# A two-layer graph kernel: the last feature chain in a fixed order, and ring places by age

## The chip, the cores and the metric

The kernel runs on one NeuronCore of a Trainium2 chip. The metric is the time of one execution on the device in microseconds (us), as the median of several runs. Lower is better. The engines are PE (TensorE: matmuls, with PEld for its weight loads), DVE (VectorE), ACT (ScalarE), POOL (GpSimd) and SP (SyncE, which here issues all the transfers). Each engine works through its own instructions in order; semaphores tie the engines together.

## The reference

There are 4096 nodes with 64 features each, and a dense 4096 x 4096 matrix `adj` in which about one entry in 128 is not zero.

```python
# layer 0: two hops with tanh
h = jnp.maximum(_layernorm(x), 0.0)
for k in range(2):
    agg = adj @ h
    h = jnp.tanh(jnp.concatenate([agg, h], axis=1) @ W[k])
x = x + h
# layer 1: each row weights its last 100 nonzeros by powers of 1/2, by rank
h = jnp.maximum(_layernorm(x), 0.0)
support = h @ weight
mask = (adj != 0)
rank = jnp.cumsum(mask, axis=1); deg = rank[:, -1:]; k = jnp.minimum(deg, 100.)
pos = rank - (deg - k)
w = mask * jnp.where(pos > 0, 0.5 ** (k - pos), 0.0)
x = x + w @ support + bias
```

So `adj` (64 MB in float32) takes part three times: in hop 1, in hop 2, and in layer 1 through the ranks of its nonzeros alone. Hop 2 needs hop 1's result, and layer 1 needs that of hop 2.

## The kernel before, in words

The nodes are cut into four chunks of 1024 (`NCH`), each of eight blocks of 128. All products are computed transposed: one matmul takes a block's features (64 or 128 columns) as its stationary operand and streams 512 columns of the matrix.

**Sweep 1** (up to about 195 us) reads the whole matrix, two blocks of sources at a time. PE makes hop 1 and as much of hop 2 as the order allows. DVE and ACT turn each nonzero into a byte, and a running count along the sources gives each nonzero its rank, kept as a byte "code" in SBUF, so that layer 1 needn't read the matrix again.

**Sweep 2** (`sweep2`) has three kinds of work, which one planner interleaves.

1. *Blocks.* What hop 2 still lacks, 72 blocks of 128 sources x 1024 targets, is read again, 512 KB per block, by SP (line 813), and multiplied (line 256, two matmuls a block, which the profile records as four). The blocks of target chunks 3 and 2 come first (24 blocks), then 24 of chunk 1, then 24 of chunk 0. A block lands in one of the places of a ring. There are six places, `ring_all`; from block 20 on there are four (`slots`), since the other two become buffers for layer-1 weights. Blocks take the places in turn, `slots[seq % len(slots)]`, and a transfer can't be issued before PE has read the block that had the place. SP issues strictly in order.
2. *The feature chain* of a chunk (`finish_x2`, a generator with four stops), once its last block is in: ACT copies the sums (S, line 540); PE multiplies them with the hop's weights (py, 548); DVE adds (554); ACT takes tanh (558); DVE adds the residual, sums and centres (561, 189, 190); ACT squares (191); DVE sums and scales (193, 194); POOL takes the power -1/2 (195); DVE normalises and splits the features into a high and a low part (198, 582, 583: `feat`); POOL adds the bias (587). The work between two stops goes into the engines' queues together, and what the planner puts in between stands between them in the queues.
3. *Layer 1.* There are 128 units of work (target chunk g, source chunk J, block n of eight), in the order J = 3, 2, 1, 0. A unit needs a weight tile (128 x 1024) made from the codes. `convert` makes it, either by one exponential on ACT (line 656) or by two operations on DVE (648 and 651). PE then makes two matmuls (695) of `feat` of source chunk J with it, so a unit must wait for the features of its source chunk. After eight units the sums of a target chunk are added to `parts` in SBUF (`evict`, lines 724 to 731), and for J = 0 they are multiplied by the layer's weights (746), added (751) and stored (753). The last 56 units (`n_late`) are left for the time after the last block, 24 of them with J = 1 and 32 with J = 0, and the 32 need the features of chunk 0.

The planner is Python at build time. It keeps a clock for each engine, adds an assumed duration for every piece (`use`), and from these clocks decides what comes next: `fill` puts pairs of units into gaps in which it expects PE to wait for a block, `decode` makes weights ahead of need as long as ACT's clock is not over PE's by more than `state["lead"]`, or, for DVE, PE's by more than 1.0, and as long as a next step of the chain isn't held up (`end`). What it decides is fixed in the program; at run time every engine just follows its own order. After the last block a loop makes a chain step when it is due, then a unit if its features are ready on the clock, and `decode` after each.

Of the kernel before, what the change touches and what calls it, by code (L numbers as in the profile page):

```python
# [43 lines left out]
def gnn_kernel(  # L44
# [46 lines left out]
    def place(shape, dtype, tag, name):  # L91
        return cpool.tile(shape, dtype, tag=tag, name=name)
# [404 lines left out]
    clock = {"PE": 0.0, "DVE": 0.0, "ACT": 0.0, "POOL": 0.0, "DMA": 0.0}  # L497

    def use(engine, us, after=0.0):
        clock[engine] = max(clock[engine], after) + us  # L500
        return clock[engine]
# [97 lines left out]
    def space(ap, t=0.0, until=None):  # L599
        if until is not None:  # L600
            lent[until] = ap
        if not any(ap is v for v in gone):
            spaces.append((ap, t))
# [5 lines left out]
    def pair_space(tag, *ts):  # L609
        v = place([P, 2, CW], F32R, tag, "weights")  # L610
        for r in range(2):
            space(v[:, r, :], ts[r % len(ts)])
# [13 lines left out]
    ready = {}  # L626
    made = []
    done = {}
    chain = []
    state = {"done": 0, "lead": 5.0, "dve": False}  # L630

    def convert(engine=None):
        i = len(made)
# [26 lines left out]
    def decode():  # L660
        while True:
            ahead = len(made) - state["done"]
            now = clock["PE"] + state["lead"]

            end = max(chain[0][0], clock["PE"]) + 0.4 if chain and ahead > 3 else 1e9
            t = min((v[1] for v in spaces), default=1e9)
            act, dve = (max(clock[e], t) for e in ("ACT", "DVE"))
            if len(made) == len(units):
                act = dve = 1e9
            if state["dve"] and dve + 1.4 < act + 1.05 and dve <= min(clock["PE"] + 1.0, end - 1.4):  # L670
                convert("DVE")
            elif act <= min(now, end - 1.05):
                convert("ACT")
            elif settled and clock["DVE"] <= clock["PE"] + 1.5 and (
                not chain or max(clock["DVE"], clock["PE"]) <= max(chain[0][0], clock["PE"]) + 0.3
            ):
                J, g, s = settled[0]
                settle()
                done[J, g] = use("DVE", 1.25)
            else:  # L680
                return

    def layer1(n):

        for i in range(state["done"], min(state["done"] + n, len(units))):
            state["done"] += 1
            while len(made) <= i:
                convert()
            J, g, k = units[i]
            if k == 0 and g not in sums:  # L690
                sums[g] = pacc.tile([P, NC, C], F32, tag="acc", name="accl")
            first, last = k == 0 and (J + 1, g) not in kept, k == CB - 1 and (J, g) not in kept
            w = made[i][0]
            for c in range(NC):
                nc.tensor.matmul(  # L695
                    sums[g][:, c, :], feats[J][:, k, :], w[:, c * C : (c + 1) * C],
                    start=first, stop=last,
                )
            space(w, use("PE", 0.45, max(made[i][1], ready[J])) + 0.2)
            if k < CB - 1:  # L700
                continue
            t = clock["PE"] + 0.2

            if (J, g) == (NCH - 1, 1):

                give_back("bits")
                state["dve"] = True
            if 0 < J < NCH - 1 or J and g % 2:
                pair_space(f"code{g}{J}", t)
            elif J:  # L710
                parts[g // 2] = place([P, 2, NC, C], F32, f"code{g}{J}", "parts")
            if (J, g) in kept:
                continue
            t = evict(J, g, sums.pop(g))
            if J == 0:
                outs.append((t + 0.1, partial(finish_out, g, part(g))))
# [39 lines left out]
    def sweep2(acc):  # L756
        rings = sorted(range(RING // 2), key=lambda k: places[k][2])
        ring_all = [(k, r) for k in rings for r in range(2)]
        accs = {}
        space(place([P, CW], F32R, "hx0", "weights"), 0.0, "bits")  # L760
        plan = [(2, 16, 20), (3, 24, 32), (2, 20, 32), (1, 16, 32), (1, 8, 16), (0, 8, 32)]
        blocks = [(I, b) for I, b0, b1 in plan for b in range(b0, b1)]
        firsts = dict((v[0], v) for v in reversed(blocks))
        lasts = dict((v[0], v) for v in blocks)
        free = {s: 3.5 * (n // 2 - 2) for n, s in enumerate(ring_all)}
        slots = ring_all
        last = finish_last(acc)
        next(last)
        clock["DMA"] = -7.0
        total = len(blocks)  # L770
        n_late = 7 * CB

        def run_chain(now):
            if chain and chain[0][0] <= now:
                t, gen = chain.pop(0)
                t = next(gen, None)
                if t is not None:
                    chain.insert(0, (t, gen))
                return True
            return False  # L780

        def due(done_blocks):

            return (len(units) - n_late) * (done_blocks - 20) / (total - 20)

        def fill(s):

            while True:
                i = state["done"]
                if (  # L790
                    i + 2 > len(units) - n_late or units[i][0] not in ready or len(made) < i + 2
                    or max(ready[units[i][0]], made[i + 1][1]) > clock["PE"] + 0.3
                    or max(clock["DMA"], free[s]) + 1.33 + 2.2 < clock["PE"] + 0.9
                ):
                    return
                layer1(2)
                run_chain(clock["PE"])
                decode()

        seq = 0  # L800
        for n in range(0, total, 2):
            I, b = blocks[n]
            if n == 20:
                slots = ring_all[:4]
                pair_space(f"ring{rings[2]}", *(free[s] for s in ring_all[4:]))
            if I not in accs:
                accs[I] = two(name="acc1") if I == 1 else plow.tile([P, C], F32, tag="low", name="acc1")
            fill(slots[seq % len(slots)])
            for r in range(2):
                s = slots[seq % len(slots)]  # L810
                seq += 1
                a = ring[s[0]][:, s[1], :]
                nc.sync.dma_start(a, adjA[I, NB - 1 - b - r])
                landed = use("DMA", 1.33, free[s]) + 2.2
                agg_pair(accs[I], at(b + r)[:, D:], a, (I, b + r) == firsts[I], (I, b + r) == lasts[I])
                free[s] = use("PE", 0.9, landed)
            next(last, None)
            if (I, b) == (2, NB - 2):
                give_back(I)
            if (I, b + 1) == lasts[I]:  # L820
                gen = finish_x2(I, accs[I])
                chain.append((next(gen), gen))
            run_chain(clock["PE"])
            if I == 0:
                state["lead"] = 10.0
            decode()
            while state["done"] < min(due(n + 2) + 6, len(units) - n_late):
                i = state["done"]
                J = units[i][0]
                if J not in ready or max(ready[J], made[i][1] if len(made) > i else 1e9) > clock["PE"] + 0.3:  # L830
                    break
                layer1(1)
                run_chain(clock["PE"])
                decode()
        for k in rings[:2]:
            pair_space(f"ring{k}", free[k, 0], free[k, 1])
        while state["done"] < len(units) or chain or outs:
            if run_chain(clock["PE"]):
                decode()
                continue  # L840

            if len(outs) > 1 or outs and state["done"] == len(units):
                t, make = outs.pop(0)
                use("PE", 0.0, t)
                make()
                continue
            i = state["done"]
            if i < len(units) and units[i][0] in ready and ready[units[i][0]] <= clock["PE"] + 1.0:
                layer1(1)
                decode()  # L850
                continue
            decode()
            later = [x[0] for x in chain[:1]] + [t for t in ready.values()]
            clock["PE"] = min(t for t in later if t > clock["PE"])

    sweep2(sweep1())


# [25 lines left out]
```

## Time and profile before

| | us |
|---|---|
| median of 3 runs (374.27 to 376.18) | 374.89 |
| profiled execution | 377.52 |
| its span, first to last instruction | 375.6 |
| PE busy | 342.3 (91%) |
| DVE busy | 294.4 (78%) |
| ACT busy | 199.8 (53%) |
| POOL busy | 24.5 (7%) |
| mean granted PE clock | 0.979 |
| layer-1 matmuls, line 695, x254 recorded | 68.1 |
| weights on ACT, line 656, x92 | 96.8 |
| weights on DVE, lines 648 and 651, x35 each | 24.2 + 25.4 |
| block transfers of 512 KB, issue to landing (median) | 5.0 |

A row of the profile's list of groups is one line, engine and operation: its busy time, the mean of one instruction in ns, and then the idle time of the engine just before, with what ended it. In a line of the timeline, the start comes first, then the time that the merged instructions span, then engine, line, operation, tiles and number. The bracket is the idle time before it and what ended that. A wait for several semaphores is put down to the one that came last, which can be a coincidence. Times in a trace count from the span's start.

### The profile page before, as it was taken

The numbers are of one execution on the slowest core, as the hardware profiler recorded it, in microseconds if no ns is written. First come the engines' busy times: TensorE is split into PE (matmuls) and PEld (weight loads), VectorE is DVE, ScalarE is ACT, GpSimd is POOL, SyncE is SP. The second block draws the span as 40 slices with busy tenths as digits, with TensorE's granted clock in tenths as the row PEclk, the third lists the DMA queues.
The fourth block names the chain that finished last, engine by engine and source line by source line (L and its number), as shares of the span: only waits on it lengthen the run. The fifth ranks groups of instructions, "written<-read, shape, count | busy, mean of one in ns | idle before, by whom it ended". The sixth has DMA issues, their size and how long they took to land.

```text
span 375.6 us, 3973 instructions
## 1 busy us (share of the span) xinstructions
PE 342.3 (91%) x1356; PEld 154.7 (41%) x1356; DVE 294.4 (78%) x524; ACT 199.8 (53%) x226; POOL 24.5 (7%) x21
## 2 busy tenths in 40 slices
PE   3787789999999999999999987988999999995996
PEld 0242224334343443444443421323355544364785
DVE  4999989399989999799989648678167667759863
ACT  2287981674266442530004314085979299928990
POOL 2221100000000000000000004012000030003000
PEclk9999999999999999999999999799999999999798
DMA  8999999999995977849889897978877789800002
GB/s 266 412 410 408 407 411 408 409 410 409 409 367 199 374 305 251 320 171 337 296 335 315 290 366 261 344 240 286 305 257 243 258 301 306 311 38 0 3 28 84
DMA packets 29827, 108.45 MB, mean 289 GB/s; under 512 B 2416, under 2 KB 2800, under 8 KB 29808
## 3 DMA queue, kind: packets, MB, share of 16 engines
q1 hardware_dynamic: 29808, 108.21, 77.5%
q8 instruction: 10, 0.16, 0.2%
q14 instruction: 9, 0.07, 0.1%
HBM read 107.15 MB, written 1.05 MB: 288 GB/s over the span
## 4 chain that ended last, share of the span: by engine, by line
PE 72%; DMA 18%; SPq 4%; ACT 4%; issue 1%; DVE 0%; ACTq 0%
PE acc L468 22%; PE accl L695 16%; PE acc L256 15%; PE acc_low L256 10%; DMA ring<-in_adjA_dram 9%; DMA codes<-in_adjA_dram 8%; SPq L428 3%; PE po L208 3%; PE pto L746 2%; PE pt L324 2%; ACT weights L656 1%; ACT codes L229 1%; PE pt L319 1%; ACT codes L230 1%; PE py L548 1%
## 5 line engine op out<-in xcount | busy, mean ns | idle before, releaser
L656 ACT ACTIVATE weights<-codes,zero 128x1024 fp32r<-128x1024 uint8 x92 | 96.8, 1136 | 6.7 <-PE accl L695 6.2
L256 PE MATMUL acc<-ring,hx 128*64 128x512 f32 x288 | 73.7, 626 | 10.1 <-DMA ring<-in_adjA_dram 10.0
L695 PE MATMUL accl<-weights,feat 128*128 128x512 f32 x254 | 68.1, 414 | 4.2 <-ACT weights L656 4.2
L468 PE MATMUL acc<-ring,hx 128*128 128x512 f32 x152 | 66.1, 593 | 0.0
L695 PEld LDWEIGHTS accl<-weights,feat 128*128 128x128 f32 x254 | 47.2, 195 | 32.2 <-ACT weights L656 12.2
L256 PE MATMUL acc_low<-codes,hx 128*64 128x512 f32 x224 | 53.4, 599 | 7.2 <-DMA codes<-in_adjA_dram 5.5
L468 PEld LDWEIGHTS acc<-ring,hx 128*128 128x128 f32 x152 | 28.6, 190 | 37.1 <-issue 36.5
L250 DVE TENSOR_SCALAR cnt<-codes 128x512 uint16<-128x512 uint16 x128 | 37.6, 294 | 4.4
L249 DVE TENSOR_TENSOR codes<-mbuf,cnt 128x512 uint16<-128x512 uint16 x90 | 38.4, 427 | 3.1
L256 PEld LDWEIGHTS acc<-ring,hx 128*64 128x64 f32 x288 | 17.1, 139 | 53.0 <-DMA ring<-in_adjA_dram 31.7
L195 POOL TENSOR_TENSOR s<-s,half 128x8 f32<-128x8 f32 (+2 forms) x9 | 17.9, 1990 | 313.5 <-DVE s L194 313.5
L396 DVE TENSOR_TENSOR codes<-codes,after 128x2048 uint16<-128x2048 uint16 x32 | 37.7, 1218 | 0.0
L651 DVE TENSOR_SCALAR weights<-bits 128x1024 fp32r<-128x1024 f32 x35 | 25.4, 726 | 15.0 <-PE accl L695 10.8
L230 ACT ACTIVATE codes<-codes 128x1024 uint8<-128x1024 int8 x32 | 33.8, 1057 | 1.0
L256 PE MATMUL acc_low<-ring,hx 128*64 128x512 f32 x96 | 26.8, 679 | 7.9 <-DVE hx L198 6.2
L238 DVE TENSOR_SCALAR mbuf<-ring 128x2048 uint8<-128x2048 f32 x27 | 32.9, 1220 | 0.8 <-DMA ring<-in_adjA_dram 0.6
L229 ACT ACTIVATE codes<-codes 128x1024 int8<-128x1024 f32 x24 | 25.1, 1048 | 14.7 <-DMA codes<-in_adjA_dram 14.7
L256 PEld LDWEIGHTS acc_low<-codes,hx 128*64 128x64 f32 x224 | 15.2, 136 | 38.3 <-issue 25.7
L648 DVE TENSOR_SCALAR bits<-codes 128x1024 uint32<-128x1024 uint8 x35 | 24.2, 691 | 4.8 <-PE accl L695 4.0
L238 DVE TENSOR_SCALAR mbuf<-codes 128x2048 uint8<-128x2048 f32 x21 | 25.6, 1220 | 0.0
L289 ACT CAST mbuf<-mbuf 128x1024 bf16<-128x1024 uint8 x1 | 1.0, 1044 | 37.7 <-DVE mbuf L288 37.7
L724 DVE TENSOR_TENSOR parts<-accl,parts 128x512 f32<-128x512 f32 x16 | 10.3, 684 | 9.7 <-PE accl L695 9.7
(87 smaller groups left out, 244.5 us busy)
## 6 DMA issues: line engine op xcount, KB each, us to landing
ring<-in_adjA_dram SPq DMA_DIRECT2D x74, 512.0 KB, 5.0
codes<-in_adjA_dram SPq DMA_DIRECT2D x33, 1024.0 KB, 14.8
ring<-in_adjA_dram SPq DMA_DIRECT2D x30, 1024.0 KB, 6.2
pre<-in_x_dram SPq DMA_DIRECT2D x4, 256.0 KB, 7.3
xres<-in_x_dram SPq DMA_DIRECT2D x4, 256.0 KB, 5.8
out_dram<-o SPq DMA_DIRECT2D x3, 256.0 KB, 2.5
out_dram<-o SPq DMA_DIRECT2D x2, 128.0 KB, 2.0
wb<-in_weights_dram SPq DMA_DIRECT2D x1, 192.0 KB, 17.2
```

The source lines that it names most:

```text
L229: nc.scalar.activation(sign, a[:, r], AF.Sign)
L230: nc.scalar.activation(m, sign, AF.Square, scale=float((FLAG - 1 + 0.25) ** 0.5))
L238: nc.vector.tensor_scalar(m, a, 0.0, float(FLAG - 1), op0=ALU.not_equal, op1=ALU.mult)
L249: nc.vector.tensor_tensor(q, marks[r].bitcast(U16), cnt, op=ALU.add)
L250: nc.vector.tensor_scalar(cnt, q, 0x7F7F, None, op0=ALU.bitwise_and)
L256: nc.tensor.matmul(acc[c * D : (c + 1) * D, :], src, a[:, c * C : (c + 1) * C], start=first, stop=last,)
L396: nc.vector.tensor_tensor(q, q, a[:, None, :].to_broadcast([P, 4, CW // 2]), op=ALU.subtract)
L468: nc.tensor.matmul(acc[0][:, c, :], at(g), a[:, r, c * C : (c + 1) * C], start=g == CB * I - 1, stop=g == 0,)
L648: nc.vector.tensor_scalar(state["bits"], q, float(ZERO), ONE, op0=ALU.subtract, op1=ALU.mult)
L651: nc.vector.tensor_scalar(w, state["bits"].bitcast(F32), 2.0 ** (127 - LOW), None, op0=ALU.mult)
L656: nc.scalar.activation(w, q, AF.Exp, scale=LN2, bias=zero)
L695: nc.tensor.matmul(sums[g][:, c, :], feats[J][:, k, :], w[:, c * C : (c + 1) * C], start=first, stop=last,)
```

## The change

There are four edits, all in the planner of sweep 2.

1. When the ring shrinks to four places at block 20, the four are put in the order in which they were last used, and the count starts again, so block 20 takes the oldest place.
2. During the last chunk's blocks, the lead that ACT may have in making weights shrinks with the number of blocks left, at most 10 and down to nothing.
3. After the last block, the chain of chunk 0 is written out by hand: two units, one weight conversion on ACT, the chain up to tanh, three units, two conversions on ACT, two parts of the chain (up to the power on POOL), three units, and the rest of the chain.
4. After that the planner goes on with a lead of 3 for ACT and 2 for DVE, and DVE may also convert on its clock up to the moment at which the features of chunk 0 are ready.

```diff
-    state = {"done": 0, "lead": 5.0, "dve": False}
+    state = {"done": 0, "lead": 5.0, "dve": False, "dlead": 1.0, "free": 0.0}
...
-            if state["dve"] and dve + 1.4 < act + 1.05 and dve <= min(clock["PE"] + 1.0, end - 1.4):
+            if state["dve"] and dve + 1.4 < act + 1.05 and dve <= min(max(clock["PE"] + state["dlead"], state["free"]), end - 1.4):
                 convert("DVE")
...
             if n == 20:
-                slots = ring_all[:4]
+                slots = ring_all[2:4] + ring_all[:2]
+                seq = 0
                 pair_space(f"ring{rings[2]}", *(free[s] for s in ring_all[4:]))
...
             if I == 0:
-                state["lead"] = 10.0
+
+                state["lead"] = min(10.0, 1.1 * (total - 3 - n))
...
         for k in rings[:2]:
             pair_space(f"ring{k}", free[k, 0], free[k, 1])
+
+        ((_, gen),) = chain
+        chain.clear()
+        state["lead"] = 10.0
+        layer1(2)
+        convert("ACT")
+        next(gen)
+        layer1(3)
+        for _ in range(2):
+            convert("ACT")
+        next(gen)
+        next(gen)
+        layer1(3)
+        next(gen, None)
+        state.update(lead=3.0, dlead=2.0, free=ready[0])
         while state["done"] < len(units) or chain or outs:
             if run_chain(clock["PE"]):
                 decode()
```

## The prediction

> **What bounds the kernel now.** I read the page first (span 375.6 us, PE 91% busy), then the busy time in stretches of 25 us. From 75 to 200 and from 275 to 300 us PE is busy all of the time, from 300 to 325 for 24.97 of 25 us. It loses time at 200 to 275 (1.86 + 3.58 + 3.35 us) and at 325 to 350 (5.50 us): around the two places that the diff touches. Lines of PE in order of time, first hole:
>
> ```profile
> 230.37 1.08 PE L256 MATMUL acc<-ring,hx 128*64 128x512 f32 x4 [0.15 <-DMA ring<-in_adjA_dram]
> 233.60 1.97 PE L256 MATMUL acc<-ring,hx 128*64 128x512 f32 x4 [2.15 <-DMA ring<-in_adjA_dram]
> 236.48 4.52 PE L256 MATMUL acc<-ring,hx 128*64 128x512 f32 x12 [0.91 <-DMA ring<-in_adjA_dram]
> ```
>
> One block of the second sweep is x4. Counted from 0, the lines are blocks 19, 20, and 21 to 23. Block 20 waits 2.15 us, block 21 waits 0.91, and both lines run slow: 1.97 us where a block takes 1.08, 4.52 where x12 took 2.79 at 224.89. The columns of the stretches are the stretch, its length, busy PE, PEld, DVE, ACT, POOL, then PE's clock, DMA share, GB/s:
>
> ```profile
> 234.00:236.00 2.00, 1.57 (x4) 0.00 (x0) 1.93 (x3) 0.00 (x0) 0.73 (x1) 0.50 0.88 313
> 238.00:240.00 2.00, 2.00 (x8) 0.56 (x8) 1.87 (x2) 0.00 (x0) 0.00 (x0) 0.50 0.93 364
> 348.00:350.00 2.00, 2.00 (x6) 1.52 (x6) 1.75 (x4) 2.00 (x3) 0.00 (x0) 0.50 0.03 8
> ```
>
> After each hole PE runs at half clock. Second hole, in order of time:
>
> ```profile
> 331.45 0.59 ACT L540 COPY S<-acc 128x512 f32<-128x512 f32 x1 [2.13 <-PE acc L256]
> ...
> 335.80 0.69 DVE L554 TENSOR_TENSOR y<-py,pre 128x512 f32<-128x512 f32 x1 [3.65 <-PE py L548]
> 336.40 1.28 DVE L724 TENSOR_TENSOR parts<-accl,parts 128x512 f32<-128x512 f32 x2
> ...
> 340.30 26.10 ACT L656 ACTIVATE weights<-codes,zero 128x1024 fp32r<-128x1024 uint8 x25
> ...
> 343.95 1.79 DVE L651 TENSOR_SCALAR weights<-bits 128x1024 fp32r<-128x1024 f32 x1
> 345.67 0.68 DVE L198 SCALAR_TENSOR_TENSOR xc<-xc,s 128x512 f32<-128x512 f32 x1
> 346.38 0.43 DVE L582 TENSOR_SCALAR feat<-xc 128x512 fp32r<-128x512 f32 x1
> 346.84 0.69 DVE L583 SCALAR_TENSOR_TENSOR feat<-xc,feat 128x512 fp32r<-128x512 f32 x1
> ...
> 347.68 9.83 PE L695 MATMUL accl<-weights,feat 128*128 128x512 f32 x32 [4.18 <-ACT weights L656]
> ```
>
> The chain of chunk 0's features runs from the last block (T = 331.40) to 347.53; PE idles from 343.50 to 347.68. The profile puts that on ACT, but the weights of that unit are the third of the 25 conversions, done about 343.5; the features' end fits. Then x32 takes 9.83 us where the same number at full clock takes 7.44 (x16 in 3.72), so the clock costs 2.4.
>
> **The Trainium skill.** "TensorE: Matmul & The Clock Gate", Part 1, says that PE's clock falls to half after an idle window of about 3.4 us and needs about as long busy to recover. The trace agrees on the half (0.50) and on the hole of 4.18 us, but the first fall came after only 2.15 us of idleness; so I count a gap of 2 us or more as costing clock, about 2.5 us each time as in both holes, and the 1.59 us gap before block 31, at clock 1.00, as not. "SBUF — State Buffer", SBUF: two separate sides, says that VectorE and GpSimd lock a port pair for a whole instruction; here L651 takes 1.79 us in place of 0.69 while POOL's L587 runs (343.94, 1.26 us), and L198 takes 1.74 beside it in an earlier chunk. "DMA: Bandwidth & Descriptors", Anatomy of one DMA, fits 2.0 us plus bytes over 436 GB/s, for another queue than SP: 3.2 us for 512 KB. The shortest landing of L813 is 3.2, the median 5.0.
>
> **Part 1, ring places by age.** Six places shrink to four at block 20. Before, block 20 takes the place that block 18 has just had (read until 230.2), so its transfer is issued at 230.25 and lands at 233.55; 21 waits for 19, and 22 and 23, whose places are long free, queue behind them on SP. After, 20 and 21 take the places of 14 and 15, read by 225.97 and 226.83. Landings of blocks 12 to 19 are 1.27 us apart (221.42 to 230.32 in seven steps), so 20 and 21 land about 231.6 and 232.8, 22 and 23, issued when 18 and 19 end, at 234.1 and 235.4. Block 23 ends about 236.5, not 241.0. No operation is added; the order of units and blocks behind it moves, because the planner's clock does. The gaps stay under 0.3 us, so I take the clock as full.
>
> From there to block 41 (274.70 before) the waits before were 2.15 + 0.91 + 1.27 + 0.17 + 1.59 + 0.14 + 0.17 = 6.4 us and the slow clock 0.89 + 1.73 = 2.6, together 9.0. After, stepping on with 0.93 us a block, 0.465 a unit (x16 in 3.72 is eight units) and 3.3 to 5.7 us from issue to landing, I find: blocks 20 to 23 wait 0.7, 24 and 25 (now ahead of the first units, behind a 256 KB residual load) 1.1, 30 and 31 1.6, 36 to 41 0.2: 3.6. That leaves 5.4. From there to T PE waited only for blocks 57 (0.03), 70 and 71 (0.64 + 0.69), and the last pattern stays. In the new order blocks 52 to 55 stand together with one pair of units behind them, so a place is asked for again after some 3.7 us where landing takes 3.3 to 5.2: waits of about 0.5 before 54 and 55 and 1.0 before 56 and 57. **T comes 5.4 - 1.5 = 3.9 us earlier.** Bounds: 0 if landings of 5 us after issue fill every new gap; 6.5 if hardly a new gap opens; a gap of 2 us would take 2.5 more.
>
> **Part 2, the chain in fixed order.** Before, T to the end of the span is 375.60 - 331.40 = 44.2 us. After, PE has 2 units, py, then 3 + 3. In us after T: S 0.64; py 0.93 to 1.95; y 2.64; tanh 3.30; pre, sum and xc 5.47 (0.72 each with its start; the 1.28 of L724 no longer lies between); ACT puts one conversion between S and tanh and two between tanh and square, ending at 5.45; square 6.13; sum and s 7.05; POOL 1.95 and 0.15 to reach it: 9.15, with L724 x2 in DVE's gap. Then xc: L587 starts with it, so I take 1.74, not 0.68: 10.95; L582 and L583: 12.15. Before, the same point was 16.1. The DVE conversions that stood in the chain (L648 and L651 at 339.65 to 345.7) move behind it. PE's 24 units and py need 24 x 0.465 + 0.93 = 12.1, so the hole closes, worth 4.2 plus 2.4 of clock.
>
> But 41 conversions are then still due (87 of 128 made at T) where 38 were, because the lead shrinks in the last blocks and DVE makes none until 12.15. ACT: 3 in the gaps, then 26 from 6.15 at 1.044 (25 in 26.10): the last ends at 33.4. DVE: one before T, then 11 at 1.53 (L648 at 348.97 to 350.50), with L724 x2 (1.28, two pairs) and one L751 (0.69) among them: the last at 32.2. PE, taking each unit when its weights are there, with the two readings-out of 1.82, stops briefly at the DVE ones (97, 99, 101, 112, 119) and ends its last unit at 35.3, not at 30.5 as bare work gives; before it was 368.59 - 331.40 = 37.2. Then as before 3.77 + 0.45 + 2.79 to the span's end: 42.3. **The tail gains 1.9**, with bounds 0 (another 1.9 us of conversion) and 6.7 (PE never waits: 30.5 + 7.0 = 37.5).
>
> Cost at nothing: fixing the order and naming ACT add no instruction. In T's stretch the conversions hide under PE's blocks; were that cover gone, one is 1.04 on ACT.
>
> Sum: 3.9 + 1.9 = 5.8 us off the profiled span, 375.6 to 369.8. The profiled execution took 377.52 us, 2.6 above the median; the saving taken off the median of 374.89 gives **369.1**.
>
> **Rivals.** (a) The ring gives nothing back: later landings eat it. For it: places are asked for again 3.7 us after their release, and second transfers of a pair took 4.4 to 5.9 us to land (block 29: 5.85). Against it: the 14 pairs of blocks 42 to 69 waited 0.03 us in all. Then only the tail: about 372.8. (b) Conversions don't bind the tail, if ACT and DVE run ahead further than I step: 3.9 + 6.6 = 10.5, so 364.4. Against it: ACT was busy without a break for 26.1 us before. (c) Slower: PE comes to wait on DVE's conversions in the tail. They share an in-order queue with evictions that wait for PE, and the number of units ahead falls from 13 to 17 to 4 to 8, so each wait is passed on. Before, this buffer hid them. My DVE step is (32.2 - 12.15) / 11 = 1.82 us per conversion; at 2.35 it eats the 5.8 us, and at 2.6 the time is 378. For it: DVE's evictions waited for PE for 9.7 us in all before. Against it: ACT makes 21 of the last 32 in its own queue, whatever DVE waits for. (d) Neither hole is worth much, since other waits end at the same moment: 374.
>
> **How the numbers follow.** My case 0.52 (its own range 367.0 to 371.3), (a) 0.18, (b) 0.18, (c) 0.06, (d) 0.06. Within 0.5% (1.9 us, about what this kernel's measurement can tell from no change) lie (d) and a ninth of (a): 0.08; slower 0.06; faster 0.86. The range, 363.9 to 372.9, leaves out (c), (d) and parts of (a) and (b).
>
> **What would show it.** Block 20 starts within 0.3 us of block 19, the clock stays at 1.0 from 232 to 240, block 23 ends near 236.5; short waits before blocks 31 and 54 to 57. L583 of the last chunk ends 12 us after the last block; no hole of 4 us and no half clock behind it; instead PE waits under 1 us each on DVE's L651; ACT's conversions run to 2 us before PE's last unit. I am wrong if block 24 or the pairs behind it wait as long as 20 did, if the clock halves in the tail, or if PE's last unit ends more than 37 us after T.

## The result, and the profile after

The changed kernel took 371.62 us (median; 369.38 to 374.35) against 374.71 us for the kernel before (372.32 to 379.08). The ratio is 0.9917, with a 95% interval from 0.9891 to 0.9943. The change made the kernel faster, by 3.1 us where 5.8 were forecast. The time lies inside the range, 2.5 us above the forecast, 0.3 above the top of the range that I gave for my own case, and 1.2 below rival (a).

| us | before | after |
|---|---|---|
| profiled execution | 377.52 | 370.68 |
| its span | 375.6 | 368.8 |
| T, end of the last block | 331.40 | 327.41 |
| last L583 of the features, after T | 16.13 | 12.01 |
| PE's last unit, after T | 37.19 | 34.33 |
| end of the span, after T | 44.19 | 41.35 |
| mean granted PE clock | 0.979 | 1.000 |

The two profiled executions differ by 6.8 us and the medians by 3.1. The profiled execution of before was 2.8 us slower than its median; the next section argues that this excess lies ahead of T. (The rows after T are taken from the end times of single instructions in the trace.)

PE in order of time, around the switch from six places to four:

```profile
229.80 1.08 PE L256 MATMUL acc<-ring,hx 128*64 128x512 f32 x4 [0.22 <-DMA ring<-in_adjA_dram]
231.06 2.31 PE L256 MATMUL acc<-ring,hx 128*64 128x512 f32 x8 [0.18 <-DMA ring<-in_adjA_dram]
233.53 1.08 PE L256 MATMUL acc<-ring,hx 128*64 128x512 f32 x4 [0.16 <-DMA ring<-in_adjA_dram]
235.82 1.08 PE L256 MATMUL acc<-ring,hx 128*64 128x512 f32 x4 [1.22 <-DMA ring<-in_adjA_dram]
237.80 1.08 PE L256 MATMUL acc<-ring,hx 128*64 128x512 f32 x4 [0.90 <-DMA ring<-in_adjA_dram]
```

These are blocks 19, 20 and 21, 22, 23 and 24. The wait of 2.15 us before block 20 is gone, and block 23 ends at 236.90, not 241.0. But PE still stops: 1.22 us before block 23 and 0.90 before block 24. The busy times by stretch (the columns are those of the prediction's table):

```profile
234.00:236.00 2.00, 0.78 (x6) 0.18 (x4) 1.93 (x4) 0.00 (x0) 0.10 (x1) 1.00 0.99 354
238.00:240.00 2.00, 1.85 (x8) 0.20 (x4) 0.00 (x0) 0.00 (x0) 0.00 (x0) 1.00 1.01 412
348.00:350.00 2.00, 2.00 (x10) 1.24 (x9) 2.00 (x4) 2.00 (x3) 0.00 (x0) 1.00 0.00 0
```

The third column from the right, PE's clock, was 0.50 in all three before and is 1.00 now. PE in the tail, from the last block on:

```profile
326.33 1.08 PE L256 MATMUL acc<-ring,hx 128*64 128x512 f32 x4 [0.17 <-DMA ring<-in_adjA_dram]
...
329.23 10.62 PE L695 MATMUL accl<-weights,feat 128*128 128x512 f32 x44
340.00 2.00 PE L695 MATMUL accl<-weights,feat 128*128 128x512 f32 x6 [0.16 <-ACT weights L656]
342.26 1.20 PE L695 MATMUL accl<-weights,feat 128*128 128x512 f32 x4 [0.26 <-DVE weights L651]
343.72 2.72 PE L695 MATMUL accl<-weights,feat 128*128 128x512 f32 x10 [0.26 <-DVE weights L651]
346.78 3.31 PE L695 MATMUL accl<-weights,feat 128*128 128x512 f32 x12 [0.34 <-DVE weights L651]
```

The hole of 4.18 us is gone. In its place PE waits five times for conversions, 0.16 to 0.34 us each and 1.2 in all, in four of these lines and a later one. The other engines in the tail, DVE and then ACT:

```profile
336.46 1.78 DVE L198 SCALAR_TENSOR_TENSOR xc<-xc,s 128x512 f32<-128x512 f32 x1 [0.64 <-POOL s L195]
338.27 0.43 DVE L582 TENSOR_SCALAR feat<-xc 128x512 fp32r<-128x512 f32 x1
338.73 0.69 DVE L583 SCALAR_TENSOR_TENSOR feat<-xc,feat 128x512 fp32r<-128x512 f32 x1
339.34 0.69 DVE L648 TENSOR_SCALAR bits<-codes 128x1024 uint32<-128x1024 uint8 x1
```

```profile
327.46 0.59 ACT L540 COPY S<-acc 128x512 f32<-128x512 f32 x1 [4.76 <-PE acc L256]
...
333.61 27.13 ACT L656 ACTIVATE weights<-codes,zero 128x1024 fp32r<-128x1024 uint8 x26
```

The features end at 339.42, which is T + 12.0, and DVE's conversions begin right behind them. ACT converts 26 times without a break until 360.74, T + 33.3: it is busy until 1.0 us before PE's last unit ends (361.74).

### The profile page after: what moved, and what is told of

Read it like the earlier page. It is cut to its first block, busy times and chain, and to the rows that moved or that the text cites. A ratio compares the mean times of both kernels' runs of the same rounds, so it can differ in the third digit from the quotient of the medians.

```text
span 368.8 us, 3974 instructions
## 1 busy us (share of the span) xinstructions
PE 338.8 (92%) x1356; PEld 151.4 (41%) x1356; DVE 293.0 (79%) x522; ACT 200.9 (54%) x227; POOL 24.6 (7%) x21
## 5 line engine op out<-in xcount | busy, mean ns | idle before, releaser
L656 ACT ACTIVATE weights<-codes,zero 128x1024 fp32r<-128x1024 uint8 x93 | 98.5, 1138 | 5.7 <-PE accl L695 5.2
L256 PE MATMUL acc<-ring,hx 128*64 128x512 f32 x288 | 71.6, 608 | 8.8 <-DMA ring<-in_adjA_dram 8.6
L695 PEld LDWEIGHTS accl<-weights,feat 128*128 128x128 f32 x254 | 44.9, 188 | 29.2 <-ACT weights L656 13.4
L256 PE MATMUL acc_low<-ring,hx 128*64 128x512 f32 x96 | 25.5, 643 | 8.0 <-DVE hx L198 6.3
L651 DVE TENSOR_SCALAR weights<-bits 128x1024 fp32r<-128x1024 f32 x34 | 23.6, 694 | 6.6 <-PE accl L695 3.6
L468 PE MATMUL acc<-codes,hx 128*128 128x512 f32 x40 | 17.8, 595 | 0.0
```

The source lines that it names most:

```text
L256: nc.tensor.matmul(acc[c * D : (c + 1) * D, :], src, a[:, c * C : (c + 1) * C], start=first, stop=last,)
L468: nc.tensor.matmul(acc[0][:, c, :], at(g), a[:, r, c * C : (c + 1) * C], start=g == CB * I - 1, stop=g == 0,)
L651: nc.vector.tensor_scalar(w, state["bits"].bitcast(F32), 2.0 ** (127 - LOW), None, op0=ALU.mult)
L656: nc.scalar.activation(w, q, AF.Exp, scale=LN2, bias=zero)
L695: nc.tensor.matmul(sums[g][:, c, :], feats[J][:, k, :], w[:, c * C : (c + 1) * C], start=first, stop=last,)
```

## The experiments

Two readings had to be told apart, for each half of the sum. **Ring:** the prediction says that order by age is worth 3.9 us of T; rival (a) says that it only moves waits. **Tail:** the prediction says that conversions set its length once the hole is closed; the alternatives are PE's own work (b), or DVE's queue (c).

All runs in one table. "Tail" is T to the end of the span in the profiled execution. The last column is what the median says of T: the median less the tail and less the 1.9 us that an execution takes beside its span (370.68 - 368.8; 377.52 - 375.6). That is allowed, because tails repeat: the same tail program gave 41.35 and 41.33 (after, e4), 39.72 and 39.72 (e3, e5), 39.24, 39.27 and 39.28 (e6, e11, e10), in executions whose T differed by up to 1.8 us. The spread of these kernels lies ahead of T. (The tail of before was profiled once; that it repeats as well is taken over from the others.) The kernels were measured in four groups, each with the kernel before beside it, and the ratios are to that: its medians were 374.71 for after, 375.19 for e1 to e4, 375.81 for e5 to e8 and 375.36 for e9 to e12. T of before by the median is then 328.6, 329.1, 329.7 and 329.3, so differences below 1 us between groups say little.

| kernel | ring at the switch | tail edits | median us | ratio to before [95%] | tail | T by the median |
|---|---|---|---|---|---|---|
| before | old | none | 374.71 | 1 | 44.19 | 328.6 |
| after | by age | 2, 3, 4 | 371.62 | 0.9917 [0.9891, 0.9943] | 41.35 | 328.4 |
| e1_ring_only | by age | none | 376.60 | 1.0041 [1.0020, 1.0061] | 46.35 | 328.4 |
| e2_tail_only | old | 2, 3, 4 | 372.27 | 0.9936 [0.9912, 0.9960] | 40.70 | 329.7 |
| e3_lead10 | by age | 3, 4 | 370.02 | 0.9863 [0.9831, 0.9894] | 39.72 | 328.4 |
| e4_after_again | by age | 2, 3, 4 | 371.52 | 0.9894 [0.9861, 0.9928] | 41.33 | 328.3 |
| e5_lead10_no_ring | old | 3, 4 | 371.05 | 0.9884 [0.9846, 0.9921] | 39.72 | 329.4 |
| e6_dve2 | by age | 3, 4, two on DVE | 368.94 | 0.9843 [0.9800, 0.9885] | 39.24 | 327.8 |
| e7_no_share | by age | 2, 3 | 374.87 | 0.9987 [0.9958, 1.0016] | 43.87 | 329.1 |
| e8_half_loads | by age | 2, 3, 4 | 362.95 | 0.9670 [0.9626, 0.9715] | 41.34 | 319.7 |
| e9_shrink24 | six places to 24 | as e6 | 366.90 | 0.9749 [0.9717, 0.9782] | 39.75 | 325.3 |
| e10_dve2_no_ring | old | as e6 | 370.34 | 0.9849 [0.9814, 0.9885] | 39.28 | 329.2 |
| e11_dve2_again | by age | as e6 | 370.59 | 0.9840 [0.9796, 0.9883] | 39.27 | 329.4 |
| e12_share_no_chain | by age | 2, 4 | 373.33 | 0.9940 [0.9909, 0.9972] | 43.52 | 327.9 |

**e1_ring_only** is the kernel before with edit 1 alone.

```diff
-                slots = ring_all[:4]
+                slots = ring_all[2:4] + ring_all[:2]
+                seq = 0
```

> The kernel before with edit 1 alone (ring places by age at block 20). By the steps of the prediction the idle and slow-clock time around blocks 20 to 23 goes, and the last block ends about 4 us earlier than in the profile before (327.4 in place of 331.4), while the tail from there to the end keeps its 44 us. Theory A (both parts save, but the clock part of each hole is not in every execution, so medians move less than profiles): 1 to 2.5 us faster in the median. Theory B (later landings give the ring's saving back in most executions): within 0.5 us of before, with new waits behind block 23 that add up to 5 us. Theory C (only the ring saves): the whole 3.1 us of the change.

It was slower than before by 0.4%, which none of the three theories had. In its profiled execution T came at 326.19, 5.2 us earlier than in that of before; but this execution (374.50) was the fastest of its 22 and that of before a slow one, so I go by the medians. PE around its last block:

```profile
326.12 5.75 PE L695 MATMUL accl<-weights,feat 128*128 128x512 f32 x24
331.71 1.09 PE L548 MATMUL py<-wz,S 128*128 128x128 f32 x8
...
344.86 8.56 PE L695 MATMUL accl<-weights,feat 128*128 128x512 f32 x30 [5.91 <-DVE feat L583]
```

The edit moves the planner's clock, and the planner then puts twelve units (x24) ahead of py, so py starts 5.5 us after the last block (3.3 before), and PE later stands for 5.91 us until the features are there. The tail grows from 44.19 to 46.35 us. T by the median is 328.4, against 329.1 for before in the same group: the ring edit alone gained some 0.7 us in T, and it cost 2.2 us in the tail through the planner. Edit 3 takes the planner out of that place.

**e2_tail_only** is the changed kernel with the ring order of before; **e3_lead10** is the changed kernel without edit 2; **e4_after_again** is the changed kernel once more, on the same chip as these.

```diff
-                slots = ring_all[2:4] + ring_all[:2]
-                seq = 0
+                slots = ring_all[:4]
```

> The changed kernel with edit 1 undone, so edits 2 to 4 alone. The hole of 2.15 us before block 20 and the half clock behind it should be there as before, and the hole of 4.18 us before the last chunk's features gone; from the last block to the end some 42 us in place of 44.2. Theory A: 1 to 2.5 us faster in the median. Theory B: the whole 3.1 us. Theory C: within 0.5 us of before, since conversions of weights bind the tail in both.

```diff
-                state["lead"] = min(10.0, 1.1 * (total - 3 - n))
+                state["lead"] = 10.0
```

> The changed kernel with edit 2 undone (lead of 10 in the last chunk's blocks): 90 weight tiles are made before the last block in place of 87, so ACT has three conversions less to make in the tail, 3.1 us of its time. If the tail is bound by conversions, as the prediction's step says, the end comes 1 to 3 us earlier than with the change as it is, unless the copy S of the last chunk now waits behind a conversion (up to 1.05 us lost). If PE's own work binds the tail, it is the same within 0.5 us.

> The changed kernel once more, to be compared with the other three on one chip. About 371.6 us, 0.992 of before; single executions between 369 and 374.5, with the longer ones at a lower mean PE clock (0.987 to 0.994) than the shorter (0.995 to 1.0) if the clock is what spreads them.

e2 came out 2.4 us faster than before by the ratio and 2.9 by the medians, between theories A and B; its hole before block 20 is there as expected (2.20 us), its tail is 40.70 and not 42. e2 against e4 puts the ring edit at 0.0042 of the time, 1.6 us (0.75 between the medians), with intervals that overlap. In e4 the six executions show no tie between time and clock (371.05 us at 0.993, 372.21 at 0.995); of the 17 of the changed kernel in the result, the five longest have a mean clock of 0.987 to 0.994 and the five shortest 0.995 to 1.000.

e3 against e4: 370.02 and 371.52, so edit 2 costs 1.5 us (1.2 by the ratios). The tail explains that: 39.72 against 41.33. With the lead kept at 10, 90 conversions have ended at T in the trace, and 88 in e4; I had counted 87. ACT makes 27 after T, not 29, and its last one ends at T + 31.26, not 33.33. ACT needs 1.04 us for one and DVE about 1.82 (the prediction's step), so together they make one in 0.66 us by estimate; two more due are 1.3 us by that rate and 2.1 on ACT alone, and 1.6 were measured.

**e5_lead10_no_ring** is e3 with the old ring order. **e10_dve2_no_ring** and **e11_dve2_again** (e6 once more) repeat the comparison on one chip. The diff from e3 and from e11 is that of e2.

> e3_lead10 with the ring order of the kernel before, so the two differ in edit 1 alone. Theory 1, the ring edit only moves waits (what it saves at blocks 20 to 23 comes back after block 41): the same as e3_lead10 within 1 us, ratio to before 0.984 to 0.990, and in the trace blocks 20 to 23 wait about 3.1 us where e3 waited 1.24, while blocks 42 to 69 wait 0 to 0.3 us where e3 waited 1.59. Theory 2, the prediction's part 1, the ring edit is worth 3.9 us: about 374, ratio 0.997.

> e6_dve2 with the ring order of the kernel before: edit 1 undone, with the same tail, beside e11_dve2_again on the same chip. Theory 1, the ring edit is worth about 1 us net (as between e5_lead10_no_ring and e3_lead10): the time is 0.5 to 1.5 us above e11_dve2_again. Theory 2, nothing: within 0.4 us of it. The prediction's part 1: 3.9 us above it.

> e6_dve2 once more, beside e10_dve2_no_ring and e9_shrink24 on the same chip: 368.5 to 369.5, ratio to before 0.982 to 0.987.

The ring edit is worth 0.8 us by e3 and e5 (ratios 0.9863 and 0.9884) and 0.3 by e10 and e11 (0.9849 and 0.9840, here the other way round: it costs 0.3). With e2 against e4 that is -0.3, 0.8 and 1.6 us. Only the last may be told from zero, and none is near 3.9. In e5's trace blocks 20 to 23 wait 2.63 us and blocks 42 to 69 0.41; in e3's 1.24 and 1.59. The e11 median missed its expectation by 1.1 us. Where the gain goes is seen by adding up, for all profiled executions, the time between block ends (means; the four kernels with the old order, and the eight with order by age at block 20 and whole loads):

| us | old order | by age | difference |
|---|---|---|---|
| end of block 19 to end of 23 | 9.52 | 5.89 | -3.6 |
| end of 23 to end of 41 | 32.44 | 33.00 | +0.6 |
| end of 41 to T | 56.62 | 59.54 | +2.9 |
| of that, waits before blocks 42 to 69 | 0.11 | 1.58 | +1.5 |

The rest of the 2.9 is moved work: at block 41, 22 units were done with the old order and 19 by age, in every one of these executions, and 3 x 0.465 = 1.4 us. These 1.4 us are missing in the row above, so they are neither gain nor loss. What comes back is some 2.0 us between blocks 23 and 41 (0.9 of waits, 0.9 of half clock) and 1.5 of waits behind: all but 0.1 of what the switch saves. Half clock comes back like this, PE in e11 and in e5:

```profile
235.34 1.08 PE L256 MATMUL acc<-ring,hx 128*64 128x512 f32 x4 [1.27 <-DMA ring<-in_adjA_dram]
237.94 3.68 PE L256 MATMUL acc<-ring,hx 128*64 128x512 f32 x8 [1.52 <-DMA ring<-in_adjA_dram]
```

```profile
232.81 1.98 PE L256 MATMUL acc<-ring,hx 128*64 128x512 f32 x4 [2.00 <-DMA ring<-in_adjA_dram]
235.41 4.85 PE L256 MATMUL acc<-ring,hx 128*64 128x512 f32 x12 [0.62 <-DMA ring<-in_adjA_dram]
```

With the old order (e5) block 20 waits 2.00 us and four blocks run slow. By age (e11) the waits stand before blocks 23 and 24, and blocks 24 and 25 run slow, 3.68 us for x8 where full clock takes 2.31. The clock fell at block 24 or 25 in five of the eight executions with order by age (e3, e6, e7, e11, e12).

**e8_half_loads** cuts the landing time instead of the order.

```diff
-                nc.sync.dma_start(a, adjA[I, NB - 1 - b - r])
+                cut = slice(0, C if n >= 20 else CW)
+                nc.sync.dma_start(a[:, cut], adjA[I, NB - 1 - b - r][:, cut])
```

> The changed kernel, but from block 20 on a transfer brings the first half of a block's columns alone; the matmuls of the other half read what lay in the place, so half of the data of those blocks is left out of the result. The order of the work is unchanged. Theory 1, the waits before blocks 20 to 71 are bound by how long a transfer takes to land: they fall from 6.4 us in all to 1 to 2.5, the last block ends 4 to 5 us earlier and the time is about 367. Theory 2, they are bound by when a place comes free and SP issues: they fall by less than 2 us and the time stays above 369.5. The result is also the most that any order of the ring's places could still win.

```profile
229.22 3.65 PE L256 MATMUL acc<-ring,hx 128*64 128x512 f32 x16 [0.20 <-DMA ring<-in_adjA_dram]
233.70 1.08 PE L256 MATMUL acc<-ring,hx 128*64 128x512 f32 x4 [0.82 <-DMA ring<-in_adjA_dram]
```

Blocks 19 to 22 now run as one line. Waits before blocks 20 to 71 fall from 6.36 to 1.17 us, and T comes 8.4 us earlier in the profile (319.02 against 327.41), 8.7 by the medians. It is more than expected: beside the 5.2 us of waits, a block that follows another without a gap takes some 0.9 us where one that starts after a stop takes 1.08 plus its start. The tail is unchanged (41.34). (0.6 of the 8.4 us lie ahead of block 20, in the spread.) So from block 20 on this stretch hangs on the transfers, and the first theory stands. Half loads shorten both the landing of one transfer and the pace of the stream, so e8 doesn't tell these two apart.

**e9_shrink24** leaves the landing time alone and keeps more places: six until block 24, then four. (The second line of the edit keeps DVE's conversions from starting while their buffer still holds a weight tile.)

```diff
-            if n == 20:
-                slots = ring_all[2:4] + ring_all[:2]
-                seq = 0
+            if n == 24:
+                slots = ring_all[:4]
...
-            if state["dve"] and dve + 1.4 < act + 1.05 and ...
+            if state["dve"] and ("bits" in state or not any(v is lent["bits"] for v, _ in made[state["done"] :])) and dve + 1.4 < act + 1.05 and ...
```

> e6_dve2, but the ring keeps its six places until block 24 instead of 20, where the places come in order of age without any edit; the third pair of places becomes weight buffers four blocks later (units 0 to 4 have three buffers until then, as before block 20 now). Theory 1, blocks 20 to 71 are bound by how long a transfer lands after its place came free, so that what is saved at one block is waited for at a later one: blocks 20 to 23 wait under 0.5 us, later blocks wait more, and the time is that of e6_dve2 within 1 us. Theory 2, the waits at the switch are a loss of their own: the last block ends as much earlier as the waits of blocks 20 to 24 fall, about 1.5 to 3 us, and the time is 366 to 367.5.

```profile
232.29 1.08 PE L256 MATMUL acc<-ring,hx 128*64 128x512 f32 x4 [0.19 <-DMA ring<-in_adjA_dram]
233.58 1.08 PE L256 MATMUL acc<-ring,hx 128*64 128x512 f32 x4 [0.21 <-DMA ring<-in_adjA_dram]
234.86 1.08 PE L256 MATMUL acc<-ring,hx 128*64 128x512 f32 x4 [0.20 <-DMA ring<-in_adjA_dram]
236.90 2.28 PE L256 MATMUL acc<-ring,hx 128*64 128x512 f32 x8 [0.96 <-DMA ring<-in_adjA_dram]
```

Here my theory that a saving at the switch is always given back fell, and the second one held: 366.90 us, 3.7 below e11 on the same chip (3.4 by the ratios), with T at 325.3 by the median. Blocks 20 to 23 run at 1.28 us each, the pace at which transfers land one behind the other (1.27). One wait is left at the switch, 0.96 before block 24, and the clock stays full behind it. The waits before blocks 42 to 69 stay (1.69 us), but from block 20 on there are 5.15 us of waits in all and no half clock, where the eight kernels by age have 7.3 and 0.9 in the mean. The reading that fits all three (order by age, half loads, six places) is a count: blocks 20 to 25 stand alone, with no unit between them. A place is used again only after its block is read (1.08) and the next has landed (3.2 at the shortest, 5.0 in the median), some 6 us; four places then give one block per 1.5 us, six one per 1.0, which is below the pace of 1.27. (Blocks 20 to 23 took 6.02 us in the changed kernel, 1.5 each.) Order decides only before which of these blocks PE waits: the waits before blocks 20 to 25 add up to 3.2 us in the mean with either order, and to 1.9 with six places. The count is an estimate of mine. The edit also gives layer 1 its third pair of buffers four blocks later, and 17 units are done at block 41, not 19, so the places are not all that differs. That six places until block 24 gain 3 to 4 us is measured. It is the fastest version found that does all the work: 0.9749 [0.9717, 0.9782] of the time before.

**e7_no_share** takes edit 4's leads away; **e12_share_no_chain** takes edit 3 away and keeps them.

```diff
         next(gen, None)
-        state.update(lead=3.0, dlead=2.0, free=ready[0])
```

> The changed kernel without the new leads of edit 4 (lead 3 and 2, and DVE's leave up to the features' time); the planner goes on with a lead of 10 for ACT and 1 for DVE. Theory 1, the prediction: conversions bind the tail, so how they are shared matters; with fewer early ones on DVE while it waits, PE waits longer at each DVE conversion and the tail grows by 0.5 to 2 us, to 372 to 373.5. Theory 2, the sharing gives nothing beyond what the old rule does once the chain is fixed: 371.5, within 0.4 us. Rival (c) of the prediction, that the small number of units ahead makes PE wait on DVE's in-order queue: without the edit 0.5 to 1 us faster, about 370.7.

```profile
346.18 0.73 PE L695 MATMUL accl<-weights,feat 128*128 128x512 f32 x2 [0.31 <-ACT weights L656]
347.22 0.73 PE L695 MATMUL accl<-weights,feat 128*128 128x512 f32 x2 [0.31 <-ACT weights L656]
348.26 0.73 PE L695 MATMUL accl<-weights,feat 128*128 128x512 f32 x2 [0.30 <-ACT weights L656]
```

PE now takes one unit every 1.04 us, exactly ACT's pace, for eight units: the order gives them all to ACT, and what DVE converts meanwhile is needed later. The tail is 43.87, and the kernel is no faster than before. It loses more than the 0.5 to 2 us that I expected: 2.5 of tail. Edits 2 and 3 without the sharing close the hole (L583 at T + 12.01) and gain 0.3 us of tail.

```diff
-        ((_, gen),) = chain
-        chain.clear()
         state["lead"] = 10.0
-        layer1(2)
...
-        next(gen, None)
-        state.update(lead=3.0, dlead=2.0, free=ready[0])
         while state["done"] < len(units) or chain or outs:
+            if not chain:
+                state.update(lead=3.0, dlead=2.0, free=ready[0])
```

> The changed kernel without edit 3: the planner orders the chain of chunk 0 and what stands between its stops, and the leads of edit 4 come in once the chain is in the queues. Theory 1, the order of the chain decides when the features are there: the last chunk's L583 ends 15 to 17 us after the last block, PE has a hole of 3 to 5 us and half clock behind it, and since the conversions wait for nothing in that hole, the tail is 43 to 45 us and the time 373 to 375. Theory 2, the supply of weights alone sets the tail and the hole is only idle time that conversions need anyway: the tail is 41 to 42 us, as in the changed kernel, and the time 371 to 372.

```profile
344.91 2.58 PE L695 MATMUL accl<-weights,feat 128*128 128x512 f32 x10 [1.14 <-DVE feat L583]
347.79 0.73 PE L695 MATMUL accl<-weights,feat 128*128 128x512 f32 x2 [0.30 <-ACT weights L656]
```

The features end at T + 14.8 and PE waits 1.14 us for them, not 3 to 5 and with no half clock, probably because the planner, with other leads, puts its conversions elsewhere. The time, 373.33, and the tail, 43.52, are those of the first theory, but 1.96 of PE's 3.36 us of waits are for ACT's conversions again. So with edit 2 in, edit 3 gains 0.3 us of tail and edit 4 gains 0.7, where both together gain 2.84. Without edit 2 both gain 4.47 (44.19 - 39.72); what either gains alone without edit 2 was not run.

**e6_dve2** is e3 with two conversions on DVE ahead of the fixed chain, where DVE waits for py.

```diff
         state["lead"] = 10.0
+        for _ in range(2):
+            convert("DVE")
         layer1(2)
```

> e3_lead10 with two more weight conversions on DVE before the fixed chain, where DVE is idle (about 2.8 us before the last block's end to 2.1 us after it). Theory 1, conversions set the end of the tail: ACT makes two fewer in the tail, so the tail shrinks from 39.7 by 1 us (half of the two ACT conversions' 2.09 us, since DVE's order moves too) to 38.7 and the time is 369.0, ratio 0.984. Theory 2, PE's own work and its waits on DVE set it: within 0.3 us of e3_lead10. If the second conversion runs into the addition after py, the chain comes up to 1 us later and the kernel is slower than e3_lead10 by as much.

```profile
331.83 17.75 PE L695 MATMUL accl<-weights,feat 128*128 128x512 f32 x74
350.44 0.73 PE L695 MATMUL accl<-weights,feat 128*128 128x512 f32 x2 [0.86 <-DVE weights L651]
```

37 units run without a stop, and one wait of 0.86 us is left. The tail is 39.24, 0.5 us shorter than e3's; I expected 1. ACT's last conversion ends 1.04 us earlier than in e3 (T + 30.22), but PE's last unit only 0.49 (T + 32.23): PE stands for 0.86 of these 32.2 us, so nearly all of the tail is now PE's own work.

## Why the prediction was right, and where it was not

**The sign, the range and the two places** were right, and the tail went as written. That the time fell into the range owes something to luck: the range was wide enough to hold rival (a), and a tail that gave 0.9 us more than forecast made up for a part of what T didn't give. S ended at T + 0.64, as forecast; L198 took 1.78 us for the forecast 1.74; L583 ended at T + 12.01 for 12.15; ACT's last conversion at 33.33 for 33.4. PE waits under 1 us each on L651, the clock stays full. DVE's last conversion came at 31.06, not 32.2, and PE's last unit at 34.33, not 35.3. The term "the tail gains 1.9" measured 2.84. The likely reason is DVE's step per conversion, which I set at 1.82 us and which was (31.06 - 12.01) / 11 = 1.73. My count of conversions was off too: by the traces 88 were done at T and 92 before the change, so 40 were due where 36 had been, not 41 where 38 had been.

**The step that failed is "T comes 5.4 - 1.5 = 3.9 us earlier".** By the medians T came 0.2 us earlier in the pair before and after, and about 0.8 in the mean over the table's rows of each kind at whole loads (329.2 and 328.5). It is the 5.4 that was wrong, the waits and the slow clock up to block 41, and in two ways.

1. *The 9.0 us of waits and slow clock were those of one execution.* I took the saving from the profiled execution of before and subtracted it from the median. That execution was longer than the median by 2.6 us, which I had written down, and the excess was ahead of T: 331.40, where the three other executions with the old order have 328.4 in the mean. The stretch from block 23 to 41 took 1.7 us more than theirs, the time up to block 19 1.1 more, and the switch itself no more. Its waits before blocks 20 to 41 were 6.4 us and theirs 4.5 to 5.7; with the slow clock that is 9.0 against 6.2 to 7.9.
2. *The 3.6 us left after were too few.* I let blocks 20 to 23 wait 0.7 us and took the clock as full. They waited 1.70 in the changed kernel, 1.22 of it before block 23, and all blocks from 20 to 41 waited 4.2; in the other kernels by age 4.0 to 5.3, and in five of eight the clock fell at block 24 or 25. With the slow clock that is 4.2 to 6.8, 5.5 in the mean, where I had 3.6. I had moved the start of four transfers forward, and not asked how many blocks in a row four places can feed.

In the means over these executions, waits and slow clock up to block 41 fall from 7.6 to 5.5 us, by 2.1 and not by 5.4. The 1.5 us of new waits that I put before blocks 54 to 57 were right in size (1.58 against 0.11 before blocks 42 to 69). What is left, 0.6 us, agrees with the 0.8 by the medians. I had also written that I am wrong if block 24 waits as long as 20 did: it waited 0.90 us in the changed kernel, but 2.26 in e3 and 2.09 in e7, for 2.15 before block 20 in the kernel before.

**Rivals.** (a), the ring gives nothing back, was the right mechanism for the first half, to 0.8 us; its time of 372.8 (by its own sum 373.0) was 1.2 too high, mostly because the tail gave 2.84. It deserved more than 0.18. (b) fell: PE waits on conversions in the tail, 1.2 us in all, and two conversions fewer made it 1.6 us shorter (e3). (c) fell: DVE's queue held PE up for 0.34 us at most at a time in the changed kernel, and without edit 4 (e7) the tail was 2.5 us longer, not shorter. (d) came out half true: of the two holes, one is worth next to nothing to close by this edit.

**What the prediction did not price.** "Cost at nothing: fixing the order and naming ACT" is true of the instructions, but the hole's 4.2 + 2.4 us were not edit 3's to give. e7 shows that without the sharing of edit 4 the waits for conversions take all but 0.3 us of it, edit 2's cost included. And edit 2, which I counted only among the conversions due, costs 1.5 us by itself.

## What to carry over

When a profiled execution is slower than the median, look for where its excess lies before subtracting a wait from the median; a tail that repeats to 0.03 us tells how much of the spread is ahead of it. A hole in a busy engine can be closed for its length only if what feeds that engine can keep up: count the supply (here, by estimate, 0.66 us per weight tile from two engines) before pricing the hole. The ring that waits for landings here was mended by more places or by smaller transfers; its order decided only where the wait stood.

## What the runs showed of the hardware

**PE's clock went by stretches of 3.41 us, not by single gaps.** "TensorE: Matmul & The Clock Gate", Part 1, of the Trainium skill speaks of an idle window of about 3.4 us. The traces show this length, but not that all of it must be idle. In the 14 traces there are 13 spells of half clock, leaving out the one at the end of each program. Each lasted 3.41 or 6.83 us, and within a trace they start whole multiples of 3.41 us apart (before: 233.16 and 345.80, 33 x 3.413; e7: 31.22 and 239.43, 61 x 3.413). The spell at the end starts on the same grid where a trace has others (e2: 232.70 and 365.82, 39 x 3.413). So I cut each trace into windows on its grid and counted PE's idle time in them. The window in front of a spell and the window after it, in e6; then two such pairs in which the clock did not fall, in e8 and in e5 (PE's busy time is the second number of a line, its clock the third from the right):

```profile
234.63:238.04 3.41, 1.46 (x6) 0.42 (x8) 2.07 (x3) 0.58 (x1) 0.00 (x0) 1.00 1.00 347
238.04:241.45 3.41, 3.41 (x10) 1.00 (x7) 0.00 (x0) 0.00 (x0) 0.00 (x0) 0.50 0.96 356
```

```profile
216.89:220.30 3.41, 1.65 (x10) 0.22 (x6) 2.32 (x3) 0.58 (x1) 0.00 (x0) 1.00 0.85 335
220.30:223.71 3.41, 3.23 (x18) 1.41 (x18) 0.00 (x0) 0.00 (x0) 0.00 (x0) 1.00 1.02 417
```

```profile
324.92:328.33 3.41, 2.14 (x10) 0.43 (x6) 0.94 (x2) 2.68 (x3) 0.00 (x0) 1.00 0.65 216
328.33:331.74 3.41, 2.83 (x15) 1.86 (x16) 0.00 (x0) 1.63 (x2) 0.00 (x0) 1.00 0.02 8
```

In the 13 windows in front of a spell PE was idle for 1.84 to 2.33 us. In sweep 2, no window at full clock that kept it had more than 1.76. This sorts gaps that their length alone does not. A gap of 1.76 us in e6 shares its window with another wait (1.95 together), and the clock fell; one of 1.76 in e8 stands alone in its window, and it did not. The 1.85 us before block 71 in e5 are cut in two by the end of a window (1.27 in the first). In e11 a gap of 1.27 and the first 0.56 of the next one share a window. One window of sweep 1 (the changed kernel, at 27.7 us, 1.92 idle) does not fit (the clock is on record from 10 to 15 us on), and the grid lies elsewhere in every trace. So for this kernel a gap of some 2 us is a risk and not a fixed price.

**DVE and POOL shut each other out.** "SBUF — State Buffer", SBUF: two separate sides, of the Trainium skill says that the two engines lock a shared pair of ports for a whole instruction. The traces agree: in e12, where POOL's L587 (339.70, 1.28 us) ran beside an L651 (339.71), that L651 took 1.81 us and L198 0.68; in the changed kernel L198 took 1.78 and each L651 about 0.69. In these traces the delay of some 1.1 us fell on whichever of the two DVE had beside the POOL addition, so its price depends on what stands there.
